# A decoder layer on one core: the recurrence's powers on 128 rows, V by 128 rows, and three pieces of work at another place

## The chip, the cores and the metric

The kernel runs on one core of one Trainium2 chip. Its time is the device time of one execution in microseconds (us), the median of several runs. An execution under the hardware profiler gives the page and the trace. The engines are PE (TensorE: matrix products; PEld is its loading of weights), DVE (VectorE), ACT (ScalarE), POOL (GpSimd) and SP (SyncE, which here issues the DMAs). Everything is computed in 32-bit floats.

## What is computed

A decoder layer with three parts, each fed by a normed copy of x and added to x. x has the shape (4, 2048, 512): 4 time steps t, 2048 columns of a batch, 512 features.

```python
# 1: a linear recurrence over the 4 time steps, on 8 blocks of 64 features, complex state z
u  = einsum('hk,tbpk->tbph', Vinv * dt[:, None], layernorm(x))
for t in range(4):
    z = V @ (A * z + u[t])               # A = exp((Lambda_real + i Lambda_imag) * dt)
    y[t] = 2 * real(z)
x = x + y
# 2: attention over a context of 77 rows, 16 heads of 32
Q, K, V = layernorm(x) @ Wq.T, ctx @ Wk.T, ctx @ Wv.T
x = x + softmax(Q K^T / sqrt(32)) V @ Wo.T
# 3: up to 2048, butterfly, gelu, butterfly, down to 512
h = butterfly(layernorm(x) @ W_exp + b_exp, up_weights)
h = butterfly(gelu(h + up_bias), down_weights)
x = x + h @ W_con + b_con + down_bias
```

The recurrence is linear, so y[t] is a sum over earlier steps: y[t] = sum over s of G[t-s] xn[s], with four real matrices G[j] = 2 real(V (A V)^j Vinv dt) of 64 x 64. They are called the taps.

## The kernel before

**Units.** The 2048 columns are 16 units of 128; a unit is 4 x 128 rows of 512 features. For each unit a generator `front(u, ...)` does parts 1 and 2 and the norm of part 3; `feed_forward(u, ...)` does part 3. Units are pipelined: while `feed_forward(u)` runs, its `step()` (L785) takes pieces of `front(u + 1)`, each piece ending at a `yield`. There are 98 steps in a unit; `step()` spreads 56 pieces over them. For unit 0 the first 8 steps take none (`lead`).

**Preparation.** Before the first unit's part 3, the butterflies are multiplied into the two weight matrices (`_prepare`), the taps are made (`_recurrence_taps`, L192), keys and values are made from the context (`_keys_values`, L261), and `front(0)` runs too. These are generators; lines L970 to L1024 call them in an order written out by hand. The block stands under a manual schedule for PE, SP and POOL: these three engines keep the written order. The order of DVE and ACT, and all engines' order after the preparation, is found by a planner (PE's stays written for the first four p of unit 0). `tc.keep_in_program_order` binds single instructions.

**Taps** (L192 to L258). Real and imaginary parts stand in separate [64, ...] tiles. `vec` has three columns; a chain of small DVE operations makes dt and A from it (`_exp`, L172, twice). `pz` holds the current power of the recurrence, real and imaginary part. Each step j makes G[j] with two products into `ps_g` (L237, L238), then the next power with four products into `ps_rr` and `ps_ri` (L247 to L250) and four DVE operations that multiply by A (L253 to L256). A product of 32-bit floats is two passes of PE in the trace.

**Keys and values.** K comes for all four t at once (L275). V comes for each t apart: 77 rows, four products into `ps_v` (L285), one copy by ACT into `vsb[:, t, :]` (L287).

**Norms.** `norm_stats` (L532) reads 4 rows' statistics (`bn_stats`, L537, bound to the written order) and then finds 1/sqrt(var + eps) by a chain of 13 small DVE operations (L543 to L550, the "root"). `normed` (L558) calls it, lets `steps` pieces pass (`yield`), writes normed rows into `xn` (two buffers), transposes them on PE (L581) and copies them out on ACT (L582). `normed_pairs` does this for the first norm, with rows `xp` in the same two buffers and transposes at L614; its rows for unit 1 are written by ACT (L602). Unit 1's first statistics are made in the preparation, at loop step n = 19 (L1001).

**Part 3.** For each p of 8, `up_head`, `up_mid` and `up_tail` do the seven products of a Strassen step (L802); `up_weights(p)` loads their weights (L1039; for p = 0 and 1 two loads in the preparation, L1021 and L1018). The down weights are used as sums (`_right_sums`, L132: 18 sums of tiles for each of four blocks j; POOL does them at L141, and for the last two blocks DVE does 8 of the 18 at L143), made into two ring buffers and stored to memory (L153). Block 0's are made in the preparation; blocks 1 to 3 during p = 0 to 2 of unit 0. `ybias` = b_con + down_bias is loaded at the preparation's end (L1025, L1026), with `db` in an `xn` buffer, summed on POOL (L1027), and added to x from p = 6 of unit 0 on (L874).

Of the kernel before, what the change touches and what calls it, by code (L numbers as in the profile page):

```python
# [11 lines left out]
F32 = mybir.dt.float32  # L12
# [159 lines left out]
def _exp(nc, pool, out, x, n):  # L172

    k = pool.tile([NS, n], F32, tag=f"exp_k{n}", name="exp_k")
    r = pool.tile([NS, n], F32, tag=f"exp_r{n}", name="exp_r")
    p = pool.tile([NS, n], F32, tag=f"exp_p{n}", name="exp_p")
    ki = pool.tile([NS, n], I32, tag=f"exp_i{n}", name="exp_i")
# [14 lines left out]
def _recurrence_taps(nc, pool, psum, ssm_vec, ssm_vt, ssm_vinv, gt):  # L192


    vec = pool.tile([NS, 3], F32, name="vec")
    vt = pool.tile([NS, 3, NS], F32, name="vt")
    pz = pool.tile([NS, 2, 2 * NS], F32, tag="pz", bufs=2, name="pz")
    nc.sync.dma_start(out=vec, in_=ssm_vec)
    yield
    nc.sync.dma_start(out=vt[:, 0:2, :], in_=ssm_vt)  # L200
    nc.sync.dma_start(out=pz, in_=ssm_vinv)
    yield

    e = pool.tile([NS, 2], F32, name="e")
    _exp(nc, pool, e, vec[:, 0:2], 2)
    dt = e[:, 0:1]
    th = pool.tile([NS, 2], F32, name="th")
# [3 lines left out]
    mag = pool.tile([NS, 1], F32, name="mag")  # L211
    _exp(nc, pool, mag, th[:, 0:1], 1)

    k = pool.tile([NS, 1], F32, name="k")
    r = pool.tile([NS, 2], F32, name="r")
# [8 lines left out]
    sn = pool.tile([NS, 2], F32, name="sn")  # L224
    nc.scalar.activation(sn, r, AF.Sin)
    az = pool.tile([NS, 2], F32, name="az")
# [5 lines left out]
    nc.vector.tensor_scalar(vt[:, 2, :], vt[:, 1, :], -1.0, None, ALU.mult)  # L232
    nc.vector.tensor_scalar(pz, pz, dt, None, ALU.mult)
    nc.gpsimd.memset(gt, 0.0)
    for j in range(T):
        ps = psum.tile([P, 512], F32, tag="c", name="ps_g")
        nc.tensor.matmul(ps[:, 0:NS], lhsT=pz[:, 0, :], rhs=vt[:, 0, :], start=True, stop=False)  # L237
        nc.tensor.matmul(ps[:, 0:NS], lhsT=pz[:, 1, :], rhs=vt[:, 2, :], start=False, stop=True)  # L238
        for h in range(2):
            if j + h < T:  # L240
                q = slice(h * NS, (h + 1) * NS)
                nc.vector.tensor_scalar(gt[q, j + h, :], ps[q, 0:NS], 2.0, None, ALU.mult)
        if j == T - 1:
            break
        rr = psum.tile([P, 512], F32, tag="f", name="ps_rr")[0:NS, 0 : 2 * NS]
        ri = psum.tile([P, 512], F32, tag="f", name="ps_ri")[0:NS, 0 : 2 * NS]
        nc.tensor.matmul(rr, lhsT=vt[:, 0, :], rhs=pz[:, 0, :], start=True, stop=False)  # L247
        nc.tensor.matmul(rr, lhsT=vt[:, 2, :], rhs=pz[:, 1, :], start=False, stop=True)
        nc.tensor.matmul(ri, lhsT=vt[:, 0, :], rhs=pz[:, 1, :], start=True, stop=False)
        nc.tensor.matmul(ri, lhsT=vt[:, 1, :], rhs=pz[:, 0, :], start=False, stop=True)  # L250
        nxt = pool.tile([NS, 2, 2 * NS], F32, tag="pz", bufs=2, name="pz_next")
        ti = pool.tile([NS, 2, 2 * NS], F32, tag="ti", name="ti")
        nc.vector.tensor_scalar(ti[:, 0, :], ri, az[:, 1:2], None, ALU.mult)  # L253
        nc.vector.scalar_tensor_tensor(nxt[:, 0, :], rr, az[:, 0:1], ti[:, 0, :], ALU.mult, ALU.subtract)
        nc.vector.tensor_scalar(ti[:, 1, :], rr, az[:, 1:2], None, ALU.mult)
        nc.vector.scalar_tensor_tensor(nxt[:, 1, :], ri, az[:, 0:1], ti[:, 1, :], ALU.mult, ALU.add)  # L256
        pz = nxt
        yield  # L258


def _keys_values(nc, psum, ctx_t, wk_t, wv_t, kbd, vsb, room):  # L261
# [20 lines left out]
    for b in range(T):  # L282
        ps = psum.tile([P, 512], F32, tag="c", name="ps_v")
        for c in range(NC):
            nc.tensor.matmul(ps[0:NK, :], lhsT=ct[:, c, b * NK : (b + 1) * NK], rhs=wv[:, c, :],  # L285
                             start=c == 0, stop=c == NC - 1)
        nc.scalar.copy(vsb[:, b, :], ps[0:NK, :])  # L287
        yield

# [213 lines left out]
def kernel(ctx: ExitStack, tc: tile.TileContext, x, ctx_t, ssm_vec, ssm_vt, ssm_vinv, wq_t, wk_t, wv_t,  # L503
# [28 lines left out]
    def norm_stats(xt, keep=lambda i: i):  # L532
# [10 lines left out]
        nc.vector.tensor_scalar(v, mv[:, :, 1], LN_EPS, None, ALU.add)  # L543
        nc.vector.tensor_scalar(vi, v.bitcast(I32), 1, None, ALU.logical_shift_right)
        nc.vector.tensor_scalar(y.bitcast(I32), vi, -1.0, 1597463007.0, ALU.mult, ALU.add)
        nc.vector.tensor_scalar(v, v, -0.5, None, ALU.mult)
        for _ in range(3):
            nc.vector.tensor_tensor(w, y, v, ALU.mult)
            nc.vector.tensor_tensor(w, w, y, ALU.mult)
            nc.vector.scalar_tensor_tensor(y, w, 1.5, y, ALU.add, ALU.mult)  # L550
# [83 lines left out]
    def front(u, xt, res, wq=None):  # L634
# [15 lines left out]
        yield from normed(xt, got, 2, u == 1)  # L650
# [122 lines left out]
    def feed_forward(u, xt, rhs, other):  # L773
# [9 lines left out]
        lead = 0 if u else 8  # L783

        def step():  # L785
            slot[0] += 1
            past = slot[0] - lead
            for _ in range(max(past, 0) * 56 // (98 - lead) - max(past - 1, 0) * 56 // (98 - lead)):
                next(other, None)
# [163 lines left out]
    with ExitStack() as stack, tc.manual_schedule(engines={E.PE, E.SP, E.Pool}):  # L953
# [12 lines left out]
        keys = _keys_values(nc, psum, ctx_t, wk_t, wv_t, kbd, vsb, room)  # L966
# [32 lines left out]
        for n, _ in enumerate(prep):  # L999
            if n == 19:  # L1000
                stats[1] = norm_stats(xts[1], tc.keep_in_program_order)  # L1001
# [118 lines left out]
```

## Time and profile before

| | us |
|---|---|
| median of 3 runs | 2611.87 |
| the runs | 2610.6 to 2618.56 |
| the profiled execution, its own time | 2615.02 |
| its span on the core | 2613.2 |

| engine | busy us | share |
|---|---|---|
| PE | 2537.3 | 97% |
| PEld | 2130.7 | 82% |
| DVE | 1478.2 | 57% |
| ACT | 1126.2 | 43% |
| POOL | 923.9 | 35% |

Times inside the profile are us from the span's start. A row of the order of time reads: start, duration, engine, line, operation, out<-in, shape, count, and in brackets how long the engine was idle before it and what ended that. "PEclk" is the share of the full clock that PE was granted. In an answer by stretches each engine has its busy time and count. The preparation ends at about 199 us, where unit 0's first up product starts; from about 373 us on each unit takes about 153 us.

### The profile page before, as it was taken

What the parts mean: (1) busy time and instruction counts of PE and PEld (TensorE: products, weight loads), DVE (VectorE), ACT (ScalarE), POOL (GpSimd) and SP (SyncE); (2) the same over time, 40 slices, a digit from 0 to 9 for tenths busy, and PEclk for the clock granted to TensorE, in tenths of its full rate; (3) what the DMA queues carried; (4) which work ended last, traced back from release to release, by engine and by line L of the source; (5) the groups of instructions that cost most, each with busy time, mean ns of one, the idle gap of its engine ahead of it and who ended that gap; (6) DMA issues with size and microseconds to landing.
All of it is one profiled execution on the core that took longest, in us unless ns stands there. A gap on an engine that the chain in (4) does not pass through costs nothing.

```text
span 2613.2 us, 39583 instructions
## 1 busy us (share of the span) xinstructions
PE 2537.3 (97%) x14280; PEld 2130.7 (82%) x14280; DVE 1478.2 (57%) x3458; ACT 1126.2 (43%) x3403; POOL 923.9 (35%) x885
## 2 busy tenths in 40 slices
PE   8888999999999999999999999999999999999999
PEld 5766888887878888788887878888787878878788
DVE  6664465655646565564656556465655646465543
ACT  2453625336362542626254262624436262443621
POOL 4435421514224151422415242241524224142434
PEclk9998999999999999999999999999999999999999
DMA  5728444544645354464535446453444635444456
GB/s 179 257 80 298 159 153 149 165 163 137 224 135 178 136 171 161 138 218 141 185 134 165 170 138 218 141 186 133 158 177 137 218 133 173 147 151 174 138 187 239
DMA packets 143220, 440.70 MB, mean 169 GB/s; under 512 B 20658, under 2 KB 48434, under 8 KB 140210
## 3 DMA queue, kind: packets, MB, share of 16 engines
q1 hardware_dynamic: 143026, 438.18, 49.2%
q8 instruction: 114, 1.87, 0.3%
q14 instruction: 80, 0.65, 0.1%
HBM read 398.27 MB, written 39.86 MB: 168 GB/s over the span
## 4 chain that ended last, share of the span: by engine, by line
PE 80%; ACT 8%; DVE 7%; DMA 3%; POOL 1%; issue 1%; SPq 0%; ACTq 0%; POOLq 0%
PE ps_a L899 13%; PE ps_b L802 11%; PE ps_a L802 8%; PE ps_q L629 7%; PE ps_c L802 7%; PE ps_b L899 6%; PE ps_w L629 6%; PE ps_c L899 5%; ACT pr L700 4%; PE ps_s L644 3%; PE ps_sc L695 3%; PE ps_pt L714 3%; PE ps_o L726 2%; PE ps_t L581 2%; DMA arena<-dn 2%; DVE sw L737 1%
## 5 line engine op out<-in xcount | busy, mean ns | idle before, releaser
L855 POOL TENSOR_TENSOR arena<-arena 128x512 f32<-128x512 f32 x448 | 593.0, 1333 | 1454.5 <-ACT arena L807 784.5
L807 ACT ACTIVATE arena<-arena,hbias 128x256 f32<-128x256 f32 x384 | 193.2, 507 | 340.6 <-DVE arena L842 265.8
L700 ACT ACTIVATE pr<-ps_sc,low 128x77 f32<-128x77 f32 x960 | 297.1, 334 | 27.8 <-DVE low L698 26.9
L802 PE MATMUL ps_b<-arena 128*128 128x256 f32 x1128 | 292.6, 380 | 2.4 <-DVE arena L833 2.4
L802 PEld LDWEIGHTS ps_b<-arena 128*128 128x128 f32 x1128 | 208.9, 190 | 30.0 <-DVE arena L833 2.8
L899 PE MATMUL ps_a<-arena 128*128 128x256 f32 x896 | 220.9, 379 | 0.0
L700 ACT ACTIVATION_READ_ACCUMULATOR pr<-ps_sc,low 128x1 f32 x960 | 205.8, 214 | 0.0
L899 PE MATMUL ps_b<-arena 128*128 128x256 f32 x768 | 198.9, 380 | 0.3 <-DMA arena<-dn 0.3
L802 PE MATMUL ps_a<-xnt,arena 128*128 128x256 f32 x752 | 196.3, 380 | 0.0
L698 DVE TENSOR_REDUCE low<-ps_sc 128x4 f32<-128x308 f32 x240 | 114.8, 478 | 137.9 <-PE ps_sc L695 132.4
L899 PEld LDWEIGHTS ps_a<-arena 128*128 128x128 f32 x896 | 166.8, 190 | 25.9
L695 PE MATMUL ps_sc<-kbd,qt 128*128 128x308 f32 x480 | 169.1, 439 | 0.0
L899 PE MATMUL ps_a<-w,arena 128*128 128x256 f32 x640 | 159.3, 383 | 5.8 <-ACT arena L807 5.8
L818 ACT COPY arena<-ps_a 128x256 f32<-128x256 f32 x128 | 48.2, 376 | 268.0 <-PE ps_a L802 268.0
L802 PEld LDWEIGHTS ps_a<-xnt,arena 128*128 128x128 f32 x752 | 143.3, 191 | 22.1 <-issue 0.2
L714 PE MATMUL ps_pt<-ident,pr 128*77 128x128 f32 x1024 | 153.3, 279 | 4.8 <-DVE pt L719 4.3
L714 PEld LDWEIGHTS ps_pt<-ident,pr 128*77 128x77 f32 x1024 | 119.1, 147 | 42.7 <-DVE pt L719 16.0
L629 PE MATMUL ps_q<-xnt,wq 128*128 128x256 f32 x640 | 151.2, 379 | 2.2 <-POOL xnt L674 2.2
L899 PEld LDWEIGHTS ps_b<-arena 128*128 128x128 f32 x768 | 137.7, 190 | 15.7 <-issue 0.9
L899 PEld LDWEIGHTS ps_a<-w,arena 128*128 128x128 f32 x640 | 119.6, 191 | 26.5 <-ACT arena L807 11.4
L629 PEld LDWEIGHTS ps_q<-xnt,wq 128*128 128x128 f32 x640 | 121.4, 190 | 19.1 <-POOL xnt L674 2.6
L570 ACT ACTIVATE xn<-xt,mv,y 128x512 f32<-128x512 f32 x48 | 37.8, 811 | 225.6 <-DVE mv L555 225.6
(236 smaller groups left out, 4920.4 us busy)
## 6 DMA issues: line engine op xcount, KB each, us to landing
arena<-dn SPq DMA_DIRECT2D x256, 512.0 KB, 4.1
w<-dn SPq DMA_DIRECT2D x160, 512.0 KB, 3.5
arena<-up SPq DMA_DIRECT2D x79, 896.0 KB, 4.5
wq<-wq SPq DMA_DIRECT2D x16, 1792.0 KB, 8.4
w<-up SPq DMA_DIRECT2D x32, 896.0 KB, 5.2
xt<-in_x SPq DMA_DIRECT2D x11, 1024.0 KB, 5.2
dn<-arena SPq DMA_DIRECT2D x8, 1152.0 KB, 5.1
out<-xt SPq DMA_DIRECT2D x33, 256.0 KB, 2.3
```

The source lines that it names most:

```text
L581: nc.tensor.transpose(ps[:, c, :], rows[t][:, c * P : (c + 1) * P], ident)
L629: nc.tensor.matmul(tiles[key][:, r, :], lhsT=lhs(i, r, k), rhs=rhs(i, r, k), start=key == i and r == 0 and k == 0, stop=k == 1, skip_group ...
L644: nc.tensor.matmul(ps[:, 2 * i : T, f * NS : (f + 1) * NS], lhsT=xpt[:, i, c * (P // NS) + f, :], rhs=gt[:, 0 : T - 2 * i, :], start=i == ...
L695: nc.tensor.matmul(ps[:, 0 : 4 * NK], lhsT=qt[:, g, t, :], rhs=kbd[:, t, g, :], start=True, stop=True)
L698: nc.vector.tensor_reduce(low, sc, AX.X, ALU.min)
L700: nc.scalar.activation(pr[:, 4 * g + h, :], sc[:, h, :], AF.Exp, bias=low[:, h : h + 1], scale=-1.0, accum_out=sm[:, 4 * g + h : 4 * g + h ...
L714: nc.tensor.transpose(pt_ps[0:NK, j, :], pr[:, 4 * g + j, :], ident)
L726: nc.tensor.matmul(po[j * DH : (j + 1) * DH, g, :], lhsT=vsb[:, tt, h * DH : (h + 1) * DH], rhs=pts[0:NK, g, j, :], start=True, stop=True, ...
L802: nc.tensor.matmul(ps, lhsT=w[:, c, :], rhs=rhs[i - 1][:, c], start=first and c == 0, stop=c == 1, skip_group_check=True)
L807: nc.scalar.activation(out, x, AF.Gelu, bias=hbias[:, b : b + 1])
L855: nc.gpsimd.tensor_tensor(place(p), place(x), place(y), ALU.add if op == "+" else ALU.subtract)
L899: nc.tensor.matmul(ps, lhsT=left[:, j, :], rhs=pair[:, n, j, :], start=first and j == 0, stop=j == NB // 4 - 1, skip_group_check=True)
```

## The change

**Taps.** All tiles have 128 rows: the same 64 values stand twice. `v` is [128, 2, 64]: rows 0 to 63 hold the real and imaginary part of V, rows 64 to 127 the imaginary part with a minus sign and the real part. `va` is the same for V with its columns multiplied by A, made once at j = 0. `z` holds real part over imaginary part. So one product with 128 rows gives G[j], and one gives the next z; between them there is one copy out of PSUM. vec is loaded twice and V and Vinv in five loads.

**V.** The 308 context rows are taken 128 at a time (128, 128, 52): 12 products for 16, three ACT copies for four, into a stage `vst` in a buffer of the `xnt` pool; six DMAs then cut it into the four t of `vsb`. They stand where the fourth V block stood.

**Second unit's statistics.** At loop step n = 17 in place of 19, and the root's operations bound to the written order.

**Output bias.** Both loads and the POOL sum move to loop step n = 15, behind the load of unit 1's x; `db` stands in a `pr` buffer.

**Second norm.** For unit 1, 5 pieces pass in place of 2 between the second norm's statistics and its rows. So `front(1)` has 59 pieces, and unit 0's `step()` spreads 59.

```diff
@@ _recurrence_taps
+    halves = slice(0, NS), slice(NS, P)
+    for i, q in enumerate(halves):
+        nc.sync.dma_start(out=vec[q, :], in_=ssm_vec)
     yield
-    nc.sync.dma_start(out=vt[:, 0:2, :], in_=ssm_vt)
-    nc.sync.dma_start(out=pz, in_=ssm_vinv)
+    nc.sync.dma_start(out=v[halves[0]], in_=ssm_vt)
+    for i, q in enumerate(halves):
+        nc.sync.dma_start(out=v[halves[1], i, :], in_=ssm_vt[:, 1 - i, :])
+        nc.sync.dma_start(out=z[q, :], in_=ssm_vinv[:, i, :])
     yield
...
     for j in range(T):
+        m = va if j else v
         ps = psum.tile([P, 512], F32, tag="c", name="ps_g")
-        nc.tensor.matmul(ps[:, 0:NS], lhsT=pz[:, 0, :], rhs=vt[:, 0, :], start=True, stop=False)
-        nc.tensor.matmul(ps[:, 0:NS], lhsT=pz[:, 1, :], rhs=vt[:, 2, :], start=False, stop=True)
+        nc.tensor.matmul(ps[:, 0:NS], lhsT=z, rhs=m[:, 0, :], start=True, stop=True)
+        if j < T - 1:
+            pz = psum.tile([P, 512], F32, tag="f", name="ps_z")[:, 0 : 2 * NS]
+            nc.tensor.matmul(pz, lhsT=m.rearrange("p i n -> p (i n)"), rhs=z, start=True, stop=True)
+            z = pool.tile([P, 2 * NS], F32, tag="z", bufs=2, name="z_next")
+            nc.vector.tensor_copy(z, pz)
...
-        nc.tensor.matmul(rr, lhsT=vt[:, 0, :], rhs=pz[:, 0, :], start=True, stop=False)
-        nc.tensor.matmul(rr, lhsT=vt[:, 2, :], rhs=pz[:, 1, :], start=False, stop=True)
-        nc.tensor.matmul(ri, lhsT=vt[:, 0, :], rhs=pz[:, 1, :], start=True, stop=False)
-        nc.tensor.matmul(ri, lhsT=vt[:, 1, :], rhs=pz[:, 0, :], start=False, stop=True)
-        nc.vector.tensor_scalar(ti[:, 0, :], ri, az[:, 1:2], None, ALU.mult)
-        nc.vector.scalar_tensor_tensor(nxt[:, 0, :], rr, az[:, 0:1], ti[:, 0, :], ALU.mult, ALU.subtract)
-        nc.vector.tensor_scalar(ti[:, 1, :], rr, az[:, 1:2], None, ALU.mult)
-        nc.vector.scalar_tensor_tensor(nxt[:, 1, :], ri, az[:, 0:1], ti[:, 1, :], ALU.mult, ALU.add)
-        pz = nxt
+        if j == 0:
+            nc.vector.tensor_scalar(ti, v[:, ::-1, :], az[:, 1:2], None, ALU.mult)
+            nc.vector.scalar_tensor_tensor(va[:, 0, :], v[:, 0, :], az[:, 0:1], ti[:, 0, :], ALU.mult, ALU.subtract)
+            nc.vector.scalar_tensor_tensor(va[:, 1, :], v[:, 1, :], az[:, 0:1], ti[:, 1, :], ALU.mult, ALU.add)
         yield
@@ _keys_values
-    for b in range(T):
+    rows = T * NK
+    vst = stage()
+    for m in range(0, rows, P):
+        n = min(P, rows - m)
         ps = psum.tile([P, 512], F32, tag="c", name="ps_v")
         for c in range(NC):
-            nc.tensor.matmul(ps[0:NK, :], lhsT=ct[:, c, b * NK : (b + 1) * NK], rhs=wv[:, c, :],
-                             start=c == 0, stop=c == NC - 1)
-        nc.scalar.copy(vsb[:, b, :], ps[0:NK, :])
+            nc.tensor.matmul(ps[0:n, :], lhsT=ct[:, c, m : m + n], rhs=wv[:, c, :], start=c == 0, stop=c == NC - 1)
+        nc.scalar.copy(vst[0:n, m // P, :], ps[0:n, :])
         yield
+    for b in range(T):
+        first = b * NK
+        while first < (b + 1) * NK:
+            last = min((b + 1) * NK, first // P * P + P)
+            nc.sync.dma_start(out=vsb[first - b * NK : last - b * NK, b, :], in_=vst[first % P : (last - 1) % P + 1, first // P, :])
+            first = last
+    yield
@@ norm_stats
-        nc.vector.tensor_scalar(v, mv[:, :, 1], LN_EPS, None, ALU.add)
+        root = root or (lambda i: i)
+        root(nc.vector.tensor_scalar(v, mv[:, :, 1], LN_EPS, None, ALU.add))
...
@@ front
-        yield from normed(xt, got, 2, u == 1)
+        yield from normed(xt, got, 5 if u == 1 else 2, u == 1)
@@ feed_forward
-        lead = 0 if u else 8
+        lead, rate = (0, 56) if u else (8, 59)
@@ tile_decoder_kernel, the preparation's loop
-            if n == 19:
-                stats[1] = norm_stats(xts[1], tc.keep_in_program_order)
+            if n == 17:
+                stats[1] = norm_stats(xts[1], tc.keep_in_program_order, tc.keep_in_program_order)
             if n == 15:
                 xts[1] = load_x(1)
+                db = work.tile([P, NH, NK], F32, tag="pr", name="db").rearrange("p h k -> p (h k)")[:, 0:D]
+                nc.sync.dma_start(out=ybias, in_=b_con.partition_broadcast(P))
+                nc.sync.dma_start(out=db, in_=down_bias.partition_broadcast(P))
+                nc.gpsimd.tensor_tensor(ybias, ybias, db, ALU.add)
...
-        db = work.tile([P, D], F32, tag="xn", name="db")
-        nc.sync.dma_start(out=ybias, in_=b_con.partition_broadcast(P))
-        nc.sync.dma_start(out=db, in_=down_bias.partition_broadcast(P))
-        nc.gpsimd.tensor_tensor(ybias, ybias, db, ALU.add)
```

## The prediction

> **What bounds the kernel now.** I read the page's busy times and clock first, then the table of stretches, then the order of time where TensorE (PE) is idle, then the DMA queue.
>
> ```profile
> PE 2537.3 (97%) x14280; PEld 2130.7 (82%) x14280; DVE 1478.2 (57%) x3458; ACT 1126.2 (43%) x3403; POOL 923.9 (35%) x885
> PEclk9998999999999999999999999999999999999999
> ```
>
> PE is the bound: 97% busy. In the table of stretches each whole unit after 373 us has 159 to 160 us of PE in 162, at a clock of 1.00 (0.99 once), so units 2 to 15, which no edit touches, hold nothing to win. All that can move lies before about 262 us. In the same table (columns: stretch, its length, busy PE, PEld, DVE, ACT, POOL, granted clock, DMA share, GB/s):
>
> ```profile
> 158.00:175.00 17.00, 17.00 (x111) 15.46 (x110) 11.70 (x22) 4.99 (x10) 0.00 (x0) 1.00 0.38 123
> 175.00:186.00 11.00, 5.83 (x23) 3.10 (x22) 9.51 (x39) 4.75 (x9) 6.33 (x9) 0.90 0.19 75
> 186.00:199.00 13.00, 13.00 (x38) 6.72 (x37) 4.34 (x6) 8.72 (x16) 12.62 (x17) 0.83 0.80 220
> 199.00:212.00 13.00, 9.40 (x31) 7.32 (x30) 1.27 (x3) 4.57 (x9) 11.32 (x16) 0.74 0.98 348
> 212.00:235.00 23.00, 23.00 (x124) 20.49 (x123) 16.91 (x33) 9.24 (x20) 15.19 (x20) 1.00 0.84 279
> 235.00:252.00 17.00, 9.36 (x30) 6.72 (x29) 8.07 (x27) 7.26 (x13) 8.42 (x9) 0.70 1.01 372
> ```
>
> Three holes, each with a lowered clock behind it. In order of time (start, duration, and in brackets the idle time before and who ended it):
>
> ```profile
> 185.62 1.11 PE L581 MATMUL ps_t<-ident,xn 128*128 128x128 f32 x4 [5.17 <-ACT xn L570]
> 203.75 0.60 ACT L602 ACTIVATE xp<-xt,mv,y 128x256 f32<-128x256 f32 x1 [4.54 <-POOL ybias L1027]
> 205.63 2.08 PE L802 MATMUL ps_a<-xnt,w_first 128*128 128x256 f32 x4 [3.60 <-ACT arena L818]
> 237.83 1.62 PE L802 MATMUL ps_b<-arena 128*128 128x256 f32 x4 [2.43 <-DVE arena L833]
> 245.70 1.97 PE L581 MATMUL ps_t<-ident,xn 128*128 128x128 f32 x8 [4.55 <-ACT xn L570]
> ```
>
> And the beginning, which is PE work in a row with small holes:
>
> ```profile
> 15.08 0.43 PE L247 MATMUL ps_rr<-pz,vt 64*64 64x128 f32 x2
> 38.60 3.60 PE L285 MATMUL ps_v<-wv,ct 128*77 128x512 f32 x8
> 44.67 0.63 PE L614 MATMUL ps_t<-ident,xp 128*128 128x128 f32 x4 [2.04 <-DVE xp L604]
> ```
>
> **Recurrence's powers.** A step now issues 12 PE passes (two for each product), the new one 4: two for the taps, two for the next z. Step 0 runs from 14.50 to 16.10, 1.60 us; two passes take about 0.27 (14.50 to 14.77), so four take 0.55: 1.05 saved. Step 2 (22.90 to 24.50) saves the same; step 1 (18.37 to 20.63, with two waits on DVE) about 1.1, as I leave a wait of 0.6 in; step 3 (28.04, where V's first block ends, to 29.74, two waits on DVE in it) needs 0.3: 1.4. Together **-4.6**. DVE loses four operations of 0.34 a step and gains one PSUM copy of about that; that the exponentials work on 128 rows costs nothing where the row's length stays (a 64x2 and a 128x4 operation both take 0.15 to 0.16).
>
> On SP's queue vec becomes two DMAs and V and z five in place of two. The second vec stands ahead of ct and wk, which PE waits for at 7.37: one more issue of 0.56, **+0.57**. The other three push what is behind them: wv was issued at 7.25, just when the first wk landed, x at 9.31 with the second, so a DMA seems to wait for the eighth before it. By that reading wv, now the fifteenth, goes out at about 10.5, when the seventh (half of v, issued near 4.2 and some 6 on its way like vt) has landed, and lands 10.8 later at 21.3; PE gets to V at about 21.9. x lands near 23 where 21.1 was, and its rows are ready by 30, before their transposes at 32.7. Hidden, with little to spare: 0 to +2, I take 0.
>
> **V by 128 rows.** Twelve products of two passes for sixteen: one block of 8 passes less, 3.43 in the chain of waits (at 38.76). But this block covered a DVE row: the transposes of unit 0's first norm go one by one (one `xn` buffer is with the high products), 36.67 to the scan at 45.13 = 8.46. Without the block each is spaced as 36.67 to 38.10, 1.43, and the last by 1.4 to 2.6 (shared-in low product, 1.22): 4.8 to 6.0. Net **-3.1** (-2.5 to -3.7). The six DMAs that cut V apart wait on SP for the third ACT copy; behind them stand the bias load, not read before 196, and a row store that waits for ACT until 54.7 anyway. 616 KB need a few us by `out<-xt`, 256 KB in 2.3; V is first read at 126, so 80 us of cover. Beginning: +0.57 - 4.6 - 3.1 = **-7.1**, and what follows to 175 us hangs on PE and moves along.
>
> **Second unit's statistics sooner.** DVE runs the two units' root chains between one another from 175 to 184.7; unit 0's alone goes from 178.39 to 184.71. In its second norm the same chain took 54.15 to 57.33, with a copy of 1.03 in it. With POOL's sums beside it (DVE operations of 0.65 to 0.72 instead of 0.15) I take 4 us from 177.0: ready at 181.0, row by ACT (0.82) at 181.9 for 185.62. So -3.7, and the half clock behind the hole goes: two transpose-and-product steps took 185.62 to 190.68, 5.06, where the next took 1.29 each: -2.5. **-6.2** (-3 to -7.5). The moved statistics stand at about 164.7, and x of unit 1 (issued 158.83, landed 5.8 later) lands at 164.6: no wait, no room either. The 13 root operations fall in a stretch where DVE is idle 5.3 of 17.
>
> **Output bias sooner.** ACT stood 4.54 at a row of unit 1 because `db` held the `xn` buffer until POOL's sum; PE's 3.60 hung on that. Gone, with the half clock: three groups from 205.63 to 211.12, 5.49, are 2.59 at the 0.86 a group of later: **-6.5**. In the new place POOL is idle (22.35 before 177.72), SP has the two loads (6.89 of issue at 188.82) between x and `w_first`, which is read at 199, and the `pr` buffer was let go at 150. Cost 0; if cover fails, `w_first` has 30 us.
>
> **The clock.** The Trainium skill's page "TensorE: Matmul & The Clock Gate", Part 1, lets the full clock return after one busy window of about 3.4 us, hence 1.7 lost a stall. The rows show longer: 2.5 and 2.9, and after 245.7 a clock of about half until 252. I take the rows; by the page the two holes would be 1.9 less. The same rule speaks against the change where a new wait is long, as next.
>
> **Second norm later, and what stands behind it.** Its idle times, 2.43 and 4.55, look like the next gain. But p = 4's up weights come late:
>
> ```profile
> 188.82 6.89 SPq L1025 DMA_DIRECT2D ybias<-in_b_con  x1
> 202.52 32.61 SPq L153 DMA_DIRECT2D dn<-arena  x9
> 235.23 1.55 SPq L1039 DMA_DIRECT2D arena<-up  x1
> ```
>
> ```profile
> arena<-up SPq DMA_DIRECT2D x1, 896.0 KB, 10.1
> ```
>
> The load goes out at 235.23 after nine stores of right sums and lands at 245.3, so PE could not start p = 4 at 241 even without the transposes. PE reaching this place 12.7 earlier (6.2 + 6.5) only waits longer. What moves is the chain of POOL sums, DVE sums and stores. POOL was never long idle up to 209.85; bias sum and small waits are worth 1.1 there; the first ring's store then lands at about 208 (211.22 before; 0.5 MB of bias loads out of its way). Then POOL waited 4.11 for DVE sums at 217.16 that stood behind PSUM work of p = 1; PE is earlier, so these start at 208. With stores that land in 5 to 6 and sums of 4.4 us a ring, the last store is out at 228.6 for 234.6, the weights land at about 238.5 (bounds 233 and 243). p = 4 then starts there instead of 250.35: -11.9. Half clock for 6.8 behind a hole of some 8 us: +3.4, where before 1.65 of it lay after 250.35: -0.8. The transposes (about 2.1 of PE) lie in the hole or after it: +1.0. Sum **-8.3 for the three edits together** (-3 to -14), not 12.7 + 12. The later norm by itself is worth little: in the hole it is hidden.
>
> **Sum.** -7.1 - 8.3 = -15.4. The profiled execution took 2615.0 (span 2613.2), 3.2 above the median; carried over: 2611.9 - 15.4 = **2596.5**.
>
> **Rivals.**
> A. *The weights' wait goes too*: the order on SP is planned anew outside the preparation, and the load may pass the stores it doesn't need. Then -7.1 - 6.2 - 6.5 - 9 (the holes at 235 and 245 and their half clock, less a second of rest) = -29: 2583. For it: it needs only one block's store. Against: it stood last before. Chance 0.14.
> B. *The chain of sums doesn't move*: POOL is as busy as before and DVE's sums wait for the stores. Weights at 245.3, p = 4 there instead of 250.35: -5.05 + 3.4 - 0.8 = -2.5; with the beginning -9.6: 2602. Chance 0.17.
> C. *The change doesn't reach the beginning*: wv or x late by 4 and more through the extra issues, the sums as in B: -3 - 2.5 = -5.5 or less: 2606, within 0.3%. Chance 0.12.
> D. *Slower*: orders of DVE and ACT are planned over the whole program, so one new hole like that of 2.43 (an evacuation behind another operation) can come back in each of the 14 later units: 14 x 2.43 = 34, less 15.4: +19, 2630. It decides at 15.4 / 14 = 1.1 us a unit, and is slower by 0.3% from 1.7. Against: the units' longest holes now are 0.4 to 1.1, and their code is the same. Chance 0.09.
> The forecast 0.48, its own range 2590 to 2604.
>
> **From these** (0.3%, 7.8 us, is about what a measurement of this kernel can tell from no change): faster 0.48 + 0.14 + 0.13 of B = 0.75; within it 0.12 + 0.04 = 0.16; slower 0.09. The range leaves out D and the far end of A: 2583 to 2609.
>
> **What would show it.** Unit 0's scan near 38 instead of 45 (beginning); no wait of ACT on `ybias`; the third norm's transposes after at most 2 us of idle PE; unit 1's transposes no longer ending a wait; the p = 4 weights landing 5 to 7 us earlier against unit 0's first up product's old distance, with PE idle before them. Wrong would make it: DVE held at unit 1's statistics by x, a hole in every later unit, or up weights that overtake the stores.

## The result, and the profile after

The changed kernel takes 2605.14 us (median of 8 runs, 2602.85 to 2610.39) beside 2615.43 us for the kernel before (8 runs, 2609.82 to 2624.75): a ratio of 0.9962, interval 0.9945 to 0.9979, so about 10 us or 0.38% faster. The forecast was 15.4 us less, 2596.5. The time lies inside the range given (2583 to 2609) and 1.1 above the likeliest case's own (2590 to 2604).

The profiled execution took 2602.9 (span 2600.6; before 2615.0 and 2613.2). Busy times and clock of the page after:

```profile
PE 2527.8 (97%) x14246; PEld 2127.1 (82%) x14246; DVE 1475.5 (57%) x3452; ACT 1124.3 (43%) x3402; POOL 923.9 (36%) x885
PEclk9998999999999999999999999999999999999999
```

Nothing in these two lines tells where the time went; the same table of stretches as before does (stretch, length, busy PE, PEld, DVE, ACT, POOL, clock, DMA share, GB/s):

```profile
175.00:186.00 11.00, 9.37 (x35) 5.09 (x35) 5.19 (x10) 9.66 (x18) 9.31 (x13) 1.00 0.38 123
186.00:199.00 13.00, 12.86 (x55) 10.11 (x54) 3.50 (x8) 6.19 (x12) 12.84 (x18) 1.00 1.03 329
199.00:212.00 13.00, 8.95 (x52) 7.61 (x50) 8.82 (x14) 4.79 (x10) 12.00 (x16) 0.98 0.81 271
212.00:235.00 23.00, 16.11 (x60) 12.96 (x60) 16.10 (x43) 5.97 (x13) 10.15 (x13) 0.79 0.99 326
235.00:252.00 17.00, 16.45 (x68) 13.68 (x69) 4.46 (x10) 7.34 (x14) 6.68 (x8) 0.80 0.71 284
```

From 175 to 199 PE now runs nearly through at full clock. But 212 to 235, where PE had been busy for all of 23 us at clock 1.00, has become a stretch with 6.9 us of idle PE and a clock of 0.79. In order of time, PE after (start, duration, in brackets the idle before and who ended it):

```profile
176.68 0.66 PE L592 MATMUL ps_t<-ident,xn 128*128 128x128 f32 x4 [1.63 <-ACT xn L581]
...
213.42 2.93 PE L655 MATMUL ps_s<-gt,xpt 128*128 128x256 f32 x8 [5.47 <-ACT xpt L626]
...
228.21 1.78 PE L813 MATMUL ps_b<-arena 128*128 128x256 f32 x4 [2.17 <-DVE arena L844]
...
235.02 1.82 PE L592 MATMUL ps_t<-ident,xn 128*128 128x128 f32 x8 [3.32 <-ACT xn L581]
...
239.40 1.91 PE L813 MATMUL ps_a<-xnt,arena 128*128 128x256 f32 x4
```

The hole before the third norm is 1.63 where it was 5.17, and that of 3.60 within unit 0's first block is gone: ACT no longer waits for `ybias` before unit 1's row (4.54 before).

```profile
200.94 1.10 ACT L613 ACTIVATE xp<-xt,mv,y 128x256 f32<-128x256 f32 x2
```

The hole of 5.47 at 213 is new. The last line is the first product of p = 4 (the fifth block), 250.35 before. The beginning:

```profile
8.43 6.89 PE L276 MATMUL ps_k<-ct,wk 128*128 128x308 f32 x16 [8.43 <-DMA wk<-in_wk_t]
...
32.91 0.66 PE L625 MATMUL ps_t<-ident,xp 128*128 128x128 f32 x4
...
37.76 1.09 PE L625 MATMUL ps_t<-ident,xp 128*128 128x128 f32 x4 [1.15 <-DVE xp L615]
38.64 6.47 PE L655 MATMUL ps_s<-gt,xpt 128*128 128x256 f32 x32
```

The first transpose of unit 0's norm is 3.8 sooner (36.67 before), the scan 6.5 (45.13). And SP's queue around p = 4's weights:

```profile
196.92 28.11 SPq L153 DMA_DIRECT2D dn<-arena  x9
225.12 1.60 SPq L1051 DMA_DIRECT2D arena<-up  x1
```

Two marks cut the program for all that follows. The issue of unit 1's x load stands for the end of the beginning (158.83 before, 153.43 after). The **stage** runs from there to the issue of unit 0's last store of output (375.75 and 366.07). So the beginning gave 5.4, the stage went from 216.92 to 212.64, 4.3 less, and the units behind it gave 2.8 up to the last store of the program: 12.5 of the span's 12.6. The forecast was 7.1, 8.3 and 0.

### The profile page after: what moved, and what is told of

Same layout as the page of the kernel before. It is cut to its first block, busy times and chain, and to the rows that moved or that the text cites. A ratio compares the mean times of both kernels' runs of the same rounds, so it can differ in the third digit from the quotient of the medians.

```text
span 2600.6 us, 39527 instructions
## 1 busy us (share of the span) xinstructions
PE 2527.8 (97%) x14246; PEld 2127.1 (82%) x14246; DVE 1475.5 (57%) x3452; ACT 1124.3 (43%) x3402; POOL 923.9 (36%) x885
## 4 chain that ended last, share of the span: by engine, by line
PE 78%; ACT 9%; DVE 7%; DMA 2%; issue 2%; POOL 2%; SPq 0%; ACTq 0%; POOLq 0%; DVEq 0%
PE ps_a L910 13%; PE ps_b L813 11%; PE ps_a L813 7%; PE ps_q L640 7%; PE ps_c L813 7%; PE ps_b L910 6%; PE ps_w L640 5%; PE ps_c L910 5%; ACT pr L711 4%; PE ps_s L655 3%; PE ps_pt L725 3%; PE ps_sc L706 3%; PE ps_t L592 2%; PE ps_o L737 2%; DMA arena<-dn 2%
```

## The experiments

All were timed against the kernel before, whose median was between 2611.62 and 2615.43 in the different groups, so that times of different groups are compared by their ratios. The marks come from one profiled execution of each kernel; that of e9b_allpool_w7 was the slowest of its eleven (2616.58), that of the last run the fastest of its six (2590.03). "Load" is how long after unit 1's x load the up weights of p = 4 set out.

| run | time, us | ratio to before | x load at | stage, us | load |
|---|---|---|---|---|---|
| before | | | 158.83 | 216.92 | 76.4 |
| changed kernel | 2605.14 | 0.9962 (0.9945 to 0.9979) | 153.43 | 212.64 | 71.7 |
| e1_begin | 2606.59 | 0.9957 (0.9942 to 0.9972) | 153.21 | 216.22 | 76.3 |
| e2_bias | 2612.42 | 0.9993 (0.9984 to 1.0002) | 161.24 | 212.84 | 72.5 |
| e3_stats | 2610.87 | 0.9986 (0.9974 to 0.9998) | 157.32 | 212.32 | 72.7 |
| e4_later | 2615.47 | 0.9998 (0.9987 to 1.0009) | 160.13 | 216.75 | 76.3 |
| e5_not_later | 2603.49 | 0.9960 (0.9947 to 0.9974) | 154.00 | 212.05 | 70.9 |
| e6_no_dve_sums | 2604.00 | 0.9961 (0.9948 to 0.9973) | 156.00 | 208.99 | 71.5 |
| e7_weights_first | 2606.12 | 0.9971 (0.9963 to 0.9980) | 153.52 | 212.58 | 60.3 |
| e9b_allpool_w7 | 2609.80 | 0.9984 (0.9975 to 0.9993) | 155.73 | 215.97 | 63.3 |
| e10_w7_dve | 2602.36 | 0.9962 (0.9950 to 0.9975) | 154.24 | 206.63 | 60.4 |
| e11_w7_dve_b2 | 2600.53 | 0.9958 (0.9945 to 0.9972) | 153.80 | 208.79 | 63.3 |
| e13_all | 2597.16 | 0.9943 (0.9930 to 0.9955) | 153.71 | 205.02 | 54.3 |
| e14_stores_later | 2594.34 | 0.9934 (0.9920 to 0.9948) | 152.77 | 200.64 | 59.4 |

The mark at x moves by up to 4 us between kernels whose beginning is the same (152.77 to 156.00 in the ten with the new one, mean 154.0; 157.32 to 161.24 in the four with the old, mean 159.4), and what lies behind unit 0 by -3.9 to +5.8 (-2.8 in the changed kernel; mean of all thirteen -0.3), so the 2.8 there are not told from chance. A difference of 3 us between two times therefore says little, and the stage is the better measure for an edit within it.

### Each part alone

Kernel before with one part of the change. The beginning (taps and V):

```diff
@@ _recurrence_taps (and _exp), from the changed kernel
-        nc.tensor.matmul(ps[:, 0:NS], lhsT=pz[:, 0, :], rhs=vt[:, 0, :], start=True, stop=False)
-        nc.tensor.matmul(ps[:, 0:NS], lhsT=pz[:, 1, :], rhs=vt[:, 2, :], start=False, stop=True)
+        nc.tensor.matmul(ps[:, 0:NS], lhsT=z, rhs=m[:, 0, :], start=True, stop=True)
...
@@ _keys_values, from the changed kernel
-    for b in range(T):
+    for m in range(0, rows, P):
...
```

> The kernel before with the new taps and the new V alone. Theory 1 (the beginning is worth what the changed kernel's trace shows at 153 us, and moves everything behind it): unit 0's last store at 370.4 instead of 375.8, the whole run 5.4 us faster, the holes at 185, 205, 237 and 245 as before and each 5.4 earlier. Rival (the prediction's own size): 7.1 us. Rival 2 (something behind it keeps its time): under 3 us.

Unit 1's x is out at 153.21, 5.6 sooner (5.4 expected), and the stage is 216.22: all its holes are still there (5.17, 3.58, 2.42, 4.54). The ratio, 0.9957, is as good as that of the whole change, so in the time the other edits add nothing that these runs can tell; in the stage they give 3.6 more. 2.1 of the 8.4 us that its profile won lie behind unit 0, where no edit reaches.

The output bias:

```diff
+                db = work.tile([P, NH, NK], F32, tag="pr", name="db").rearrange("p h k -> p (h k)")[:, 0:D]
+                nc.sync.dma_start(out=ybias, in_=b_con.partition_broadcast(P))
...
-        db = work.tile([P, D], F32, tag="xn", name="db")
-        nc.sync.dma_start(out=ybias, in_=b_con.partition_broadcast(P))
...
```

> The kernel before with the output bias sooner alone. Theory 1 (the chain of right sums and their stores sets the time at which p = 3 and p = 4 can go on): ACT's wait on ybias and PE's 3.6 us go, p = 2 starts about 6.5 us sooner, but a new wait behind DVE's sums takes most of it back: unit 0's last store 1 to 3 us sooner. Rival (each hole is worth its own length): 6.5 us sooner.

The second unit's statistics:

```diff
-            if n == 19:
-                stats[1] = norm_stats(xts[1], tc.keep_in_program_order)
+            if n == 17:
+                stats[1] = norm_stats(xts[1], tc.keep_in_program_order, tc.keep_in_program_order)
```

> The kernel before with the second unit's statistics sooner alone. Theory 1: PE's hole of 5.2 us before the third norm's transposes shrinks to under 2, the first up product starts about 6 us sooner, but ACT then waits longer on ybias (POOL and SP are not sooner by more than 1.5): unit 0's last store 0 to 2 us sooner. Rival (each hole is worth its own length): 6 us sooner.

The second norm:

```diff
-        yield from normed(xt, got, 2, u == 1)
+        yield from normed(xt, got, 5 if u == 1 else 2, u == 1)
...
-        lead = 0 if u else 8
+        lead, rate = (0, 56) if u else (8, 59)
```

> The kernel before with the second norm later alone (5 pieces and rate 59). Theory 1: the up weights of p = 4 land at 245.3 as before, so the holes at 237 and 245 become one wait for them; unit 0's last store within 1.5 us of before. Rival (the hole is the norm's): the idle 2.4 and 4.5 us and their half clock go, 7 to 9 us sooner.

Statistics alone give the stage 4.6, the bias alone 4.1, and both with the rest 4.3: they are not added. Each alone gave the stage more than was expected (0 to 2 and 1 to 3) and less than its rival had (6 and 6.5); in the time, the bias alone is not clear of noise. Each closes its hole, and each time another one takes the place. PE's holes with the statistics alone and with the bias alone:

```profile
205.20 1.37 PE L803 MATMUL ps_a<-xnt,w_second 128*128 128x256 f32 x4 [4.57 <-ACT arena L819]
...
232.21 1.13 PE L803 MATMUL ps_b<-arena 128*128 128x256 f32 x4 [4.24 <-DVE arena L834]
```

```profile
221.45 1.57 PE L644 MATMUL ps_s<-gt,xpt 128*128 128x256 f32 x8 [2.66 <-ACT xpt L615]
```

With the statistics alone the hole behind ACT's wait for `ybias` grows from 3.60 to 4.57 and the one at 232 from 2.43 to 4.24; with the bias alone that of 3.60 goes, and one of 2.66 comes before the scan products, behind ACT's copy of `xpt`. What the stage gains in these four runs (0.7, 4.1, 4.6, 0.2) goes with how much sooner the load of p = 4 sets out (0.1, 3.9, 3.7, 0.1). The later norm alone is worth nothing. From these I took it that the load was the one gate; the next runs were to show it.

### The second norm back in the changed kernel

```diff
-        yield from normed(xt, got, 5 if u == 1 else 2, u == 1)
+        yield from normed(xt, got, 2, u == 1)
...
-        lead, rate = (0, 56) if u else (8, 59)
+        lead, rate = (0, 56) if u else (8, 56)
```

> The changed kernel with the second norm back at two steps of lead and the old rate, all else kept. Theory (what counts in unit 0 is when the fifth block's up weights set out, and this edit doesn't touch that): the first load of the fifth block sets out 71.7 +- 0.5 us after unit 1's x does, as in the changed kernel, and the time stays at 2605 +- 2. Rival (the holes before the norms' transposes cost by themselves): the first hole ahead of the fifth block grows by 1 to 2 us and the other from 3.3 back to 4.5, the time rises by 1.5 to 3 to about 2607.5.

The stage is 212.05 for 212.64, the time 2603.49. The holes lie elsewhere (1.90 and 0.76 near 210, then 4.02 and 4.55), their effect on the end is the same. The two ahead of p = 4 grew about as the rival had it, but the time did not rise. DVE's second four sums stand here as in the changed kernel (3.59 at 208.63), but ACT copies `xpt` before it waits for the evacuation behind them (207.62), so PE meets shorter holes there and longer ones later. So the edit costs or brings nothing that these runs can tell, as the theory had it, though the load came 0.8 sooner, not 0.5 at most.

### VectorE's sums left out

```diff
-                nc.vector.tensor_tensor(made[name], x, y, op)
+                pass
```

> The changed kernel with VectorE's sixteen sums for the down weights' combinations (line 143) left out: those combinations hold no value, so the output lacks part of the reference's computation. Theory (the new hole of 5.5 us at 213 stands there because VectorE holds at those sums, in order, while three evacuations of finished tiles are queued behind them): the hole and its half clock go, 8.4 us less up to the fourth block's first product, the fifth block's load sets out 7 to 9 us sooner after unit 1's x than 71.7 (its chain of sums loses VectorE's share too), and the time falls by 5 to 8, to 2597 to 2600. Rival (the hole is the norm's rows or the gate of the weights, not VectorE's queue): the hole stays at 4 to 6 us and the time is within 2 of 2605.

First how the hole at 213 comes about, from DVE and ACT of the changed kernel:

```profile
202.33 3.61 DVE L143 TENSOR_TENSOR arena<-arena 128x256 f32<-128x256 f32 x4 [2.58 <-DMA dn<-arena]
...
208.07 3.58 DVE L143 TENSOR_TENSOR arena<-arena 128x256 f32<-128x256 f32 x4 [1.46 <-POOL arena L141]
211.57 0.41 DVE L856 TENSOR_TENSOR arena<-ps_c,arena 128x256 f32<-128x256 f32 x1
```

```profile
212.02 0.51 ACT L818 ACTIVATE arena<-arena,hbias 128x256 f32<-128x256 f32 x1 [4.87 <-DVE arena L856]
...
212.79 0.57 ACT L626 COPY xpt<-ps_t 128x512 f32<-128x512 f32 x1
```

PE stopped at 207.95. DVE, in order, stood at the second four sums of the third block; the evacuation of a finished tile (line 856) was next in its order and came at 211.57. ACT waited 4.87 us for that, and behind two of ACT's Gelus stood the copy of `xpt`, which PE's scan products need. Without the sums (PE, then SP):

```profile
210.35 1.47 PE L655 MATMUL ps_s<-gt,xpt 128*128 128x256 f32 x8
...
228.57 1.97 PE L592 MATMUL ps_t<-ident,xn 128*128 128x128 f32 x8 [5.01 <-ACT xn L581]
...
237.41 2.07 PE L813 MATMUL ps_a<-xnt,arena 128*128 128x256 f32 x4 [3.98 <-DMA arena<-up]
```

```profile
199.49 27.87 SPq L153 DMA_DIRECT2D dn<-arena  x9
227.45 1.41 SPq L1051 DMA_DIRECT2D arena<-up  x1
```

The hole is gone, as the theory said; the time, 2604.00, is what the rival said (the theory had 2597 to 2600). Both were wrong in part. The load sets out hardly sooner (71.5 for 71.7), so DVE's sums were not what held it; PE now waits 3.98 for it, and 5.01 before the transposes. The stage is 208.99, 3.7 less than in the changed kernel; in the profiled execution (2604.00, the median itself) it is hidden because x set out 2.6 later; whether it was so in the other executions is not shown.

### The load ahead of the stores

```diff
                 _right_sums(nc, p + 1, wdn, rings, p == 0)
+                if p == 2:
+                    early.append(up_weights(4))
                 _right_stores(nc, p + 1, wdn, rings, dn26, (0, 1, 2))
```

> The changed kernel with the first load of the fifth block's up weights put on SP's queue ahead of the fourth block's stores of sums instead of behind them. Theory (those stores hold the load: the last one ahead of it then is issued at 212.7 of the changed kernel's span, the load at 213.5 instead of 225.1, and lands at 222 to 224 instead of 235.3): the hole of 3.3 us and the half clock ahead of the fifth block go, 5 to 7 us less, 2598 to 2600; the hole at 213 stays. Rival (the load isn't what sets the fifth block's start, the norm's transposes are): the load is 11 us sooner and the fifth block's first product no more than 1 us, 2604 to 2606.

The load is out at 213.84 and p = 4 begins at 228.81, 10.6 sooner than in the changed kernel, with no hole for weights or transposes before it. Yet the stage is 212.58 and the time 2606.12. The theory had 2598 to 2600; the rival had the time, but with p = 4 no more than 1 us sooner. (Lines behind 876 are two higher in this kernel.) PE, DVE and POOL:

```profile
246.45 2.08 PE L813 MATMUL ps_a<-xnt,w 128*128 128x256 f32 x4 [3.00 <-ACT arena L829]
```

```profile
244.57 0.69 DVE L671 TENSOR_TENSOR xnt<-xnt 128x512 f32<-128x512 f32 x1 [6.09 <-POOL tq L670]
245.18 0.42 DVE L856 TENSOR_TENSOR arena<-ps_c,arena 128x256 f32<-128x256 f32 x1
```

```profile
235.63 4.96 POOL L866 TENSOR_TENSOR arena<-arena 128x512 f32<-128x512 f32 x4 [12.25 <-ACT arena L818]
240.53 2.78 POOL L887 TENSOR_TENSOR xt<-xt,ybias 128x256 f32<-128x256 f32 x4
243.26 1.27 POOL L670 TENSOR_TENSOR tq<-xnt 128x512 f32<-128x512 f32 x1
```

Line 670 follows the second norm's last copy (ACT, done at 240.6), but stands on POOL behind eight operations and begins at 243.26. DVE waits at line 671 for 6.09 us, and p = 4's evacuation is queued behind it. PE had been 4.4 us ahead (the product `ps_c<-arena,w` at 242.43, in the changed kernel at 246.83); hole and half clock took it all back. So there were three things of nearly one length in this stage: the load, DVE's sums, and the additions behind the second norm. To free the load alone is worth nothing, to free DVE's sums alone was worth 3.7; the additions were not freed alone.

### All sums on POOL, and the load ahead

```diff
-            if alone or name not in FAST:
+            if True:
...
+                if p == 2:
+                    early.append(up_weights(4))
```

> As the run before, and with all of the sums for the down weights on POOL, so that VectorE has none of them in its order. Theory: sixteen sums more on POOL at 0.72 us put its chain 11.5 us later, which the load no longer waits for; the hole of 5.5 at 213 goes with its half clock, 8 us less before the fourth block, of which 3 to 7 reach the end beyond the run before: 2592 to 2597. Rival (POOL's longer chain comes out at the next thing behind the stores, the later loads of weights or unit 1's x): the hole moves there, and the time is that of the run before or up to 4 more.

The rival's number: 2609.80, 3.7 more than the run before, stage 215.97. The hole at 213 is gone, but POOL is busy from 179 on with little pause, the last of block 3's stores is issued at 231.3 in place of 224.5, and PE waits 7.64 before 229.64, for p = 4's weights, and 3.99 before 249.10. The theory had 2592 to 2597. DVE's sums have a price on DVE and, in the time of this run, a larger one on POOL; the size of the stage is that of its slowest execution.

### The additions behind the norm on VectorE

The load ahead as before, and

```diff
-        nc.gpsimd.tensor_tensor(t3, b22, b12, ALU.subtract)
+        (nc.vector if u == 1 else nc.gpsimd).tensor_tensor(t3, b22, b12, ALU.subtract)
```

> The run with the fifth block's load first, and line 670 (the first of three additions behind the second norm) on VectorE instead of POOL, for unit 1 alone. Theory (with the load early TensorE ran 4.4 us ahead of the changed kernel until VectorE, in order, stood 6.1 us at line 671 for POOL's line 670, which came 2.6 us after its input behind eight other POOL operations; the fifth block's evacuation at 245.2 was queued behind it, hole 3.0 us and half clock): the hole at 246.5 goes, unit 0's last store comes 4 to 4.5 us sooner than the 366.1 of that run, the time is 2600 to 2602. Rival (the sixth block's weights are as late, so the stage is held by its transfers): a hole of 2 to 3 us stays at the same product, now behind a load, and the time is within 1.5 of 2605.

```profile
239.79 1.17 DVE L670 TENSOR_TENSOR tq<-xnt 128x512 f32<-128x512 f32 x1 [3.40 <-ACT xnt L593]
240.88 0.41 DVE L853 TENSOR_TENSOR arena<-ps_b,arena 128x256 f32<-128x256 f32 x1
241.21 0.87 DVE L671 TENSOR_TENSOR xnt<-xnt 128x512 f32<-128x512 f32 x1
```

The hole of 3.00 is 0.69, unit 0's last store comes at 360.87, 5.2 sooner (4 to 4.5 expected), the stage is 206.63. The time, 2602.36, is 0.4 above the 2600 to 2602 expected. In the stage this confirms the third of the three. In the time the gain is not shown: the kernel before took 2611.62 in this group, and the ratio, 0.9962, is the changed kernel's own.

### Four of VectorE's sums on POOL

```diff
-            if alone or name not in FAST:
+            if alone or name not in FAST or (j == 2 and lot is RIGHT[1]):
```

> As the run before, and the second four of VectorE's sums for the third block of down weights (those that began at 208.1) on POOL instead. Theory (these 3.6 us are what the evacuations at 211.6 to 212 stood behind, so the hole of 5.5 at 213.4 comes from them alone): the hole and its half clock go, 7 us sooner at the fourth block's first product; POOL's chain is 2.9 longer, of which 2.5 fall into its wait for a store; 4 to 7 us of it reach unit 0's last store, 2594 to 2598. Rival (the fifth block's load, now out at about 216, lands near 225 and TensorE is there at 221): a new hole of 3 to 5 us with its half clock ahead of the fifth block, gain 0 to 3.

The hole at 213 goes (0.51 is left), and one of 6.90 stands at 228:

```profile
228.29 1.22 PE L813 MATMUL ps_b<-arena 128*128 128x256 f32 x2 [6.90 <-DVE arena L844]
```

```profile
220.72 3.29 DVE L143 TENSOR_TENSOR arena<-arena 128x256 f32<-128x256 f32 x4
223.93 0.68 DVE L658 TENSOR_TENSOR xt<-ps_s,xt 128x512 f32<-128x512 f32 x1
224.53 0.41 DVE L853 TENSOR_TENSOR arena<-ps_b,arena 128x256 f32<-128x256 f32 x1
```

PE comes sooner to the next block's sums, and again the evacuations (lines 853, 856 and 844) are behind them on DVE, with the next statistics between. The rival had a new hole, but for the weights; it is DVE once more. The time, 2600.53, is above the 2594 to 2598 expected and 1.8 less than without this edit, which the runs do not tell from nothing; the stage is 2.2 longer.

### The third stores behind the loads

As the last, and

```diff
-                _right_stores(nc, p + 1, wdn, rings, dn26, (0, 1, 2))
+                _right_stores(nc, p + 1, wdn, rings, dn26, (0, 1))
+            if u == 0 and p == 4:
+                for j in (1, 2, 3):
+                    _right_stores(nc, j, wdn, rings, dn26, (2,))
```

> As the run before, and the third stores of three blocks (1 MB each, the down weights as they are) set behind the loads of the fifth and sixth block instead of ahead of them. Theory (the DMA engines were busy for 97 to 104 per cent of 205 to 240 in the changed kernel, so what is queued ahead of a load delays its landing by its own time): 2 to 3 MB at 335 GB/s are 6 to 9 us that no longer lie ahead of the loads; what hole is left ahead of the fifth and sixth block goes, 2 to 4 us less than the run before. Rival (the loads wait for POOL's sums and for SP's order, not for bytes): within 1 us of the run before.

2597.16, 3.4 less than the last, stage 3.8 less: what the theory had, though the intervals of the two ratios overlap. Two of the three stores now stand behind the loads of p = 4 and p = 5, the third still before p = 5's.

Without the four sums on POOL:

> The last run without its move of VectorE's four sums to POOL: the changed kernel with the fifth block's load early, line 670 on VectorE for unit 1, and the third stores of three blocks set behind the loads. Theory (the move of sums only carried the hole of 5.5 us from 213 to one of 6.9 at 228, behind the next block's sums, and what the last run won came from the stores): the hole at 213 is there, 5 to 6 us, unit 0's last store is within 1.5 us of that run's 358.7, and the time 2596 to 2599. Rival (both edits are needed, since each alone leaves VectorE at a block's sums with the evacuations behind it): the last store comes at 360 to 362, and the time is 2600 to 2603, that of the run without either.

2594.34 us, 0.9934, the fastest of all and below the 2596 to 2599 expected; the stage is 200.64, 16.3 less than before. The hole at 213 is there (5.59), and none over 0.4 behind it up to 250. Stretches of the changed kernel, then of this one:

```profile
215.00:225.00 10.00, 10.00 (x45) 8.69 (x44) 7.50 (x14) 0.48 (x2) 7.46 (x10) 0.83 0.95 315
225.00:235.00 10.00, 4.53 (x13) 2.87 (x11) 7.26 (x27) 3.64 (x8) 2.22 (x2) 0.83 1.02 336
235.00:245.00 10.00, 9.45 (x36) 7.52 (x37) 1.72 (x3) 5.17 (x9) 6.68 (x8) 0.66 1.00 414
```

```profile
215.00:225.00 10.00, 10.00 (x50) 8.93 (x50) 8.68 (x17) 1.35 (x3) 5.06 (x7) 0.96 0.97 321
225.00:235.00 10.00, 9.56 (x48) 7.99 (x47) 5.85 (x25) 6.53 (x13) 5.88 (x7) 1.00 1.03 356
235.00:245.00 10.00, 10.00 (x52) 8.84 (x51) 4.95 (x10) 2.89 (x7) 1.92 (x2) 1.00 1.03 383
```

The DMA engines are as full in both; only the order is another, and PE and its clock are full beside them. The nearest neighbour is e10_w7_dve, which has all but the later stores: its ratio, 0.9962 (0.9950 to 0.9975), lies clear of this one, and its stage is 6.0 longer. Not all of the 6.0 is the stores': the holes of 5.51 and 2.52 in that run (before 214.29 and 346.52) are 5.59 and 2.52 here, but 6.8 and 3.4 us of half clock followed them there, 3.4 and none here, and the last section shows how that can be chance. It makes about 2.9 us (an estimate: half of PE's busy time at half clock, 5.68 and 3.16 there, 3.00 here). The last store came 5.3 sooner than the run before, more than the 1.5 either way that was expected, so in the stage the move of the four sums was a loss; the two ratios overlap. What stays open is how much of this is bytes taken from ahead of the loads, and how much is the planner's new order on DVE (block 3's first four sums now lie one by one between evacuations). Against the changed kernel itself, through the kernel before, the ratio is 0.9934 / 0.9962 = 0.9972, some 7 us; the two were not timed side by side.

## Why the prediction was right in kind and too large

**Beginning: -5.4 for -7.1.** Up to unit 0's first transpose -3.76 where 0.57 - 4.6 = -4.03 was forecast: the first K product came 1.06 later, not 0.57, and the taps gave 4.8 for 4.6. From there to the scan -2.7 for -3.1 (5.73 where I had bounds of 4.8 and 6.0). The rest, +1.1, is the scan itself, 38.64 to 45.04 in place of 45.13 to 50.46: the waits between the transposes (0.83, 0.92, 1.15) were in the sum, the half clock behind them, 37.4 to 40.8, was not. Nine of the ten profiles with the new beginning have it there, for 3.4 or 6.8 us. Over all profiles the two beginnings differ by 5.3 (154.0 and 159.4).

**Statistics and bias, each at its own hole: right.** The hole before the third norm went from 5.17 to 1.63 and its half clock is gone: -5.9 from the x load to the first up product, -6.2 forecast. ACT's wait for `ybias` went, and PE's 3.60 with it: -6.2 to the first product of p = 2, -6.5 forecast. That these 12 us would not reach the end was also forecast, and the step that was to bound them, nearly so: DVE's sums of the third block began 207.7 in the frame of that sum (202.33 + 5.4), 208 forecast; the load went out at 230.5 in it for 229.3, and landed at 240.7 (235.34 + 5.4) for 238.5, within its bounds.

**The step that failed** is "p = 4 then starts there": that PE, come early, would stand before p = 4 when the weights land, with "the transposes in the hole or after it". PE did not come early. It lost 8.4 us (of the 17.5 gained up to p = 2, 9.1 were left at p = 3) to a hole that the forecast did not have, at the very sums that I had moved forward: they were counted as the head of the chain to the load, not as an obstacle for what is queued behind them on DVE. The first products of p = 2 and p = 3, before and after:

```profile
216.16 1.03 PE L802 MATMUL ps_a<-xnt,w 128*128 128x256 f32 x4
225.27 1.03 PE L802 MATMUL ps_a<-xnt,arena 128*128 128x256 f32 x4
```

```profile
198.67 1.03 PE L813 MATMUL ps_a<-xnt,w 128*128 128x256 f32 x4
216.14 1.92 PE L813 MATMUL ps_a<-xnt,arena 128*128 128x256 f32 x4
```

So p = 4 began at 239.40, 4.1 after its weights, behind the norm's transposes at half clock; against the x load 5.6 sooner, not 11.9. The costs behind it were smaller than forecast (1.3 for 3.6), and the stage gave 4.3 for 8.3. With the sums left out the forecast's picture came true: PE waited 3.98 at p = 4 for the weights, and the stage gave 7.9. In the run with the second norm back PE's waits at this place were short (1.90 and 0.76), and it lost as much later, behind the evacuations and the norm.

**Second norm: right.** "Worth little", 0.2 alone and nothing when taken back.

**Rivals.** The measured 2605.14 is nearest to C (2606), its reason is not C's: the beginning did move. B (the chain doesn't move: stage -2.5) had the size of the stage better than the forecast, but by luck: the chain did move, by 4.7. A's load past the stores did not come by itself; put there by hand it brought nothing, where A had 9 us of it. D did not come: the units behind unit 0 scatter by a few us in total, with a mean of -0.3.

## What to carry to other kernels

When a wait is taken away, follow the engine that ran freely to the next place in each in-order queue: work moved up on one engine stands in front of whatever that engine still owes to others. If several lines of work end within a few us of each other, an edit of one can read as nothing (0.1 for the load here), and only freeing them together shows what each was worth. Measure the stage with marks, since single times hide 3 us, and compare the half clock in two stages before their lengths. Before moving sums to another engine, look at which transfers stand ahead of the loads that the next block needs.

## What was not expected of the hardware

Half clock comes in pieces of 3.4 us (3.4, 6.8, 10.2, 13.7 and 17.1 in these runs), and the same waits may or may not bring it. The three waits before unit 0's scan, 0.83, 0.92 and 1.15, in the changed kernel and in the last run (stretches around the last of them):

```profile
34.00:37.40 3.40, 1.28 (x8) 0.84 (x8) 2.65 (x7) 1.36 (x3) 0.00 (x0) 1.00 1.04 372
37.40:40.80 3.40, 3.04 (x11) 2.71 (x12) 0.21 (x1) 0.58 (x1) 0.00 (x0) 0.50 1.03 232
```

```profile
33.50:37.00 3.50, 1.28 (x8) 0.84 (x8) 2.75 (x7) 1.45 (x3) 0.00 (x0) 1.00 1.01 372
37.00:40.40 3.40, 3.06 (x20) 2.88 (x21) 0.89 (x2) 0.59 (x1) 0.00 (x0) 1.00 1.02 229
```

Half clock in the one, full in the other. The Trainium skill's page "TensorE: Matmul & The Clock Gate", Part 1, describes a window of about 3.4 us that runs freely and does not start with the kernel; that fits both the pieces and the chance. Counted back in such windows from where a later half clock begins in each run (211.48 and 212.48), one window of the changed kernel, 33.98 to 37.40, holds the three waits with 1.28 us of PE in it; in the last run they fall into two windows, with 2.23 and 1.68.

Its rule for the return, one busy window, held for the hole at 228 (half clock 228.5 to 231.9) and also for that at 213: of the two windows at half clock, the first (211.48 to 214.90) still has the end of the hole in it, with 1.48 us of PE, and the second is full. So the window in which a hole ends can count to the loss too, and the prediction's 2.5 before 190.68, which it set against 1.7 by the page, is no contradiction to it: the two windows there, 183.72 to 190.55, have 1.51 and 3.42 us of PE, and half of that is 2.5. How busy a window must be these runs leave open: behind the hole of 2.43 in the kernel before, 2.83 us of PE in 3.42 (238.33 to 241.75) brought the full clock back; behind 235.4 in the changed kernel, 2.88 (235.37 to 238.78) did not.

A sum on DVE beside a sum on POOL took 0.94 us (changed kernel, median of the 16 of line 143), alone 0.41; POOL's took 0.90 for 0.72. That doubled the block of four before the hole: 3.58 at 208.07.
